# A convolution phase: one tensor's depthwise part put off through DRAM, work dealt by estimates, norms in four pieces

## The chip, the cores and the metric

The kernel runs on one core of a Trainium2 chip. The metric is device time of one execution in microseconds (us), the median of several runs; lower is better. In the profile PE is the matrix engine (PEld its weight loads), DVE the vector engine, ACT the scalar engine, POOL the GpSimd engine, and SP the engine that issues most DMAs. Each engine works through its own instructions in a fixed order, and semaphores make one wait for another.

## The reference, cut to what matters

The program is a network of three parts: a convolutional attention layer, a two-way state-space (mamba) layer and an expert layer. Only the beginning of the first part is touched. Its input is x, 64 x 64 pixels by 256 channels, normalised in groups of channels.

```python
xc = jnp.transpose(x, (0, 3, 1, 2))
qkv = jnp.concatenate([_conv(xc, W1, 0), _conv(xc, W3, 1), _conv(xc, W5, 2)], axis=1)
qkv = _conv(qkv, Wdw, 1, groups=3 * c)
q, k, v = jnp.split(qkv, 3, axis=1)
q, k, v = (heads(q), heads(k), heads(v))     # 8 heads of 32 channels
q, k = (l2n(q), l2n(k))                      # t / max(sqrt(sum(t*t)), 1e-12) over a head's channels
attn = jnp.einsum('bhnc,bhmc->bhnm', q, k) * temperature
attn = jax.nn.softmax(attn, axis=-1)
o = jnp.einsum('bhnm,bhmc->bhnc', attn, v)
...
```

So q is a 1x1, k a 3x3 and v a 5x5 convolution with 256 channels in and out; a 3x3 depthwise convolution follows each; q and k are divided, pixel by pixel, by the norm of a head's 32 channels.

## The kernel before

`conv_phase` (L174) computes q, k and v in the first 730 us and writes them to DRAM as qd, kd and vd; the attention that follows reads them from there. Channels lie on the 128 partitions, in two tiles t = 0, 1; the image is worked on in two halves of 32 rows.

The 3x3 and 5x5 convolutions are done in a Winograd manner along a row: `weights` (L285) transforms the raw weights on DVE and stores them to DRAM (uk, uv) by POOL's queue; `inputs` (L325) transforms the normalised image xpad on DVE into nine places v; PE multiplies the transformed pieces (`feed`, L421: 6 products of 6 matmuls 128x512 for a unit of k, 8 products of 10 for a unit of v; q has 4 products of 2, straight from xpad); `transform_out` (L473) reads the products on DVE and writes pad, the convolution's output with a border. Each DVE operation of these goes through the helpers at L272 and L275, each matmul product through L452 (q L444).

A unit is one tensor, half and tile. The order is four units of k, (half 0, tile 0), (0, 1), (1, 0), (1, 1), and then q and v in turn, four of each. Below, "k0" to "k3" are the four units of k, and "v0" to "v3" the stages of one v unit with the q unit before it. The loop over units (L694 to L730) does a unit in groups of two products. At each group it reads two products, calls `tick`, does a share of the previous unit's depthwise taps, and some "fills": steps of weight and input transforms that later units need, a fixed number by tensor (`share`, L722).

`depthwise` (L507) makes the nine taps of a unit: the first on ACT (L524), eight on DVE (L528), in two pieces of 12 rows of 64 pixels (128x768) or 20 rows (128x1280) each. It reads pad and writes an accumulator acc, of which there are three. For v the result is transposed in 128x128 blocks on PE (`turn`, L581) and stored. For q and k the 512-pixel chunks go into a list, from which the norms are made three chunks at a time: `norm_sums` squares on ACT and sums each head's 32 channels with one matmul per chunk into 32 partitions of a shared bank; one tick later `norm_inverse` takes the maximum with 1e-24 (L558, DVE), the root (L559, ACT) and the reciprocal (L560, DVE) of the 96x512 tile, and one matmul per chunk spreads the result back over the 128 channels, with the temperature for q (`pick_q`); another tick later `norm_apply` (L568) multiplies, stores, and begins the next three chunks. `later` (L594) and `tick` (L597) hold this lag.

The orders on the engines are the order in which this code issues the instructions (`manual_schedule`). `feed` keeps up to three products issued ahead of the one that is read, in four PSUM banks (a_pcv), and loads the transformed weights u by SP's queue three ahead (L430). `load_raw` (L279) brings raw weights in by POOL's queue into one buffer ("wr"). A pool of six buffers (a_t) holds small temporaries: wx and wo of the weights, c (ACT's copy of a product), sq, qo and vs.

## Time and profile before

| | us |
|---|---|
| median of three runs | 4381.84 |
| the three runs | 4381.84, 4389.78, 4381.30 |
| the profiled execution | 4368.56 |
| its span on the core | 4366.8 |
| convolution phase (first attention matmul at) | 730.2 |
| attention, to about | 2018 |
| mamba, to about | 4060 |

The profiled execution is 13.3 us below the median, and 1.8 us of it lie outside the span. Mean granted clock of PE over the span is 0.904 of full speed. In the tables of instruction groups a row gives line, engine, operation, output and inputs, shapes and count, then the busy time and the mean duration of one in ns, then the idle time of the engine just before them with what ended it. In the tables of time windows a row gives for each engine its busy microseconds and, in brackets, how many instructions. In a timeline a row gives the start, the duration of a run of like instructions, and in square brackets how long the engine had been idle before and what released it.

### The profile page before, as it was taken

To read this page: it belongs to the slowest core of one execution; us is meant where nothing else is said; L and a number is where in the kernel's file an instruction comes from. 1 tells how busy PE (TensorE), PEld (TensorE's weight loads), DVE (VectorE), ACT (ScalarE), POOL (GpSimd) and SP (SyncE) were. 2 spreads that over 40 slices of the span, in tenths; PEclk is the share of its full clock that TensorE was granted. 3 is DMA by queue.
4 is the path that set the end of the run, shared out by engine and by line. 5 is a ranking of instruction groups with operands and counts; after the bars stand their busy time and mean duration, and the time that the engine had idled before them with its cause. 6 is when DMAs were issued, how large, how long until landed. Compare 5 with 4: busy or idle time off the path is not lost. (4 is left out here: it accounts for less than half of the span.)

```text
span 4366.8 us, 43278 instructions
## 1 busy us (share of the span) xinstructions
PE 3693.8 (85%) x15072; PEld 1180.6 (27%) x15072; DVE 3600.9 (82%) x2976; ACT 2685.7 (62%) x4175; POOL 1563.3 (36%) x1051
## 2 busy tenths in 40 slices
PE   4659895999999999997878788888788788876698
PEld 2224341222222222222222222222222222221243
DVE  6887876888879879778899999999999999999311
ACT  1012223888788888776677777777777777774122
POOL 2210000000000000002677677776767777776000
PEclk9879996999999999998888989989888898977799
DMA  4322223000000000003332334443323334332121
GB/s 148 125 77 93 75 79 129 4 30 11 25 23 18 16 23 18 11 23 118 104 108 98 103 124 119 123 119 107 127 82 124 124 114 118 120 109 84 63 63 37
DMA packets 150243, 351.18 MB, mean 80 GB/s; under 512 B 35461, under 2 KB 44421, under 8 KB 149502
## 3 DMA queue, kind: packets, MB, share of 16 engines
q1 hardware_dynamic: 139214, 313.17, 23.1%
q0 software_dynamic: 10800, 35.14, 2.3%
q8 instruction: 120, 1.97, 0.2%
q14 instruction: 109, 0.89, 0.1%
HBM read 268.69 MB, written 79.56 MB: 80 GB/s over the span
## 5 line engine op out<-in xcount | busy, mean ns | idle before, releaser
L1669 POOL TENSOR_TENSOR dbx<-dtxr,b 128x1024 f32<-128x1024 f32 x512 | 1205.8, 2360 | 467.7 <-DVE da L1677 320.7
L1677 DVE TENSOR_TENSOR_SCAN da<-da,state,dbx 128x1024 f32<-128x1024 f32 x512 | 1203.2, 2350 | 62.0 <-ACT state L1700 33.6
L960 ACT ACTIVATE e<-sc 128x1024 f32<-128x1024 f32 x1024 | 992.8, 1023 | 204.7 <-PE sc L953 161.2
L881 DVE TENSOR_TENSOR s<-s,e 128x1024 f32<-128x1024 f32 x768 | 880.6, 1216 | 44.7 <-ACT e L960 44.2
L1659 ACT ACTIVATE da<-dtr,aneg 128x512 f32<-128x512 f32 x1024 | 708.3, 692 | 36.0 <-DMA dtr<-dtd 3.8
L953 PE MATMUL sc<-q,kS 32*128 32x512 f32 x4096 | 653.6, 644 | 20.4 <-DMA kS<-kd 11.4
L1682 DVE TENSOR_TENSOR h<-da,c 128x1024 f32<-128x1024 f32 x512 | 627.2, 1225 | 37.7
L888 PE MATMUL av<-e,vT 128*32 128x512 f32 x4096 | 549.8, 608 | 3.7 <-ACT o L894 3.7
L1709 PE MATMUL y<-h,sel 128*32 128x512 f32 x2048 | 442.0, 675 | 130.9 <-DVE h L1682 130.7
L132 POOL TENSOR_TENSOR ln_few<-ln_few,minus_half 128x4 f32<-128x4 f32 x29 | 29.4, 1015 | 1417.8 <-DMA ln_few<-ln_row 1417.8
L452 PE MATMUL cv<-v,u 128*128 128x512 f32 x928 | 422.2, 615 | 64.4 <-DVE pad L272 27.4
L953 PEld LDWEIGHTS sc<-q,kS 32*128 32x128 f32 x4096 | 211.3, 183 | 466.9 <-issue 244.4
L1250 PE MATMUL mm<-u,win 128*128 128x512 f32 x496 | 267.2, 688 | 72.0 <-DMA u<-ud 52.4
L1700 ACT COPY state<-da 128x2 f32<-128x2 f32 x511 | 80.5, 158 | 362.5 <-DVE h L1682 360.0
L452 PEld LDWEIGHTS cv<-v,u 128*128 128x128 f32 x928 | 182.1, 198 | 302.9 <-issue 230.9
L528 DVE SCALAR_TENSOR_TENSOR acc<-pad,wdw_s,acc 128x768 f32<-128x768 f32 (+1 forms) x192 | 244.5, 1279 | 19.4 <-ACT acc L524 13.3
L1294 PE MATMUL mm<-xp,taps 128*128 128x512 f32 x480 | 221.3, 609 | 6.0 <-DVE m L1441 5.1
L881 DVE TENSOR_TENSOR s<-e 128x1024 f32<-128x1024 f32 x128 | 150.8, 1219 | 71.6 <-ACT e L960 71.4
L888 PEld LDWEIGHTS av<-e,vT 128*32 128x32 f32 x4096 | 81.3, 108 | 396.6 <-issue 379.0
L1709 PEld LDWEIGHTS y<-h,sel 128*32 128x32 f32 x2048 | 60.4, 114 | 468.5 <-DVE h L1682 292.8
L1250 PEld LDWEIGHTS mm<-u,win 128*128 128x128 f32 x496 | 104.2, 221 | 244.8 <-issue 127.0
L504 ACT COPY pad<-pad 128x480 f32<-128x480 f32 x12 | 7.1, 594 | 214.2 <-DVE pad L272 214.1
(338 smaller groups left out, 3747.3 us busy)
## 6 DMA issues: line engine op xcount, KB each, us to landing
dtr<-dtd SPq DMA_DIRECT2D x128, 512.0 KB
dtxr<-dtd SPq DMA_DIRECT2D x128, 512.0 KB
b<-bcd SPq DMA_DIRECT2D x64, 256.0 KB
c<-bcd SPq DMA_DIRECT2D x64, 256.0 KB
dtd<-dt SPq DMA_DIRECT2D x64, 256.0 KB
dtd<-few SPq DMA_DIRECT2D x64, 256.0 KB
u<-uv SPq DMA_DIRECT2D x24, 640.0 KB
u<-ud SPq DMA_DIRECT2D x16, 512.0 KB
```

What stands on the lines that cost most here:

```text
L452: nc.tensor.matmul(rows4(ps), u[:, dy, P * ci : P * ci + P], v[:, dy : dy + HR, ci, :], start=dy + ci == 0, stop=dy == k - 1 and ci == CT - 1,
L528: nc.vector.scalar_tensor_tensor(o, src, w_ap, o, ALU.mult, ALU.add)
L881: nc.vector.tensor_tensor(z, x, y, ALU.add)
L888: nc.tensor.matmul(g.av[32 * h : 32 * h + 32, :], vT[:, kb, P * t + 32 * h : P * t + 32 * h + 32], es[h // 2][:, h % 2, :], start=kb == 0, ...
L953: nc.tensor.matmul(ps[h // 2][:, h % 2, :], kS[r, t, P * kb : P * kb + P], q_t[r, t, :], start=True, stop=True,)
L960: nc.scalar.activation(e, ps[i], AF.Exp)
L1250: nc.tensor.matmul(ps, win[d][:, t, P * e : P * e + P], u[:, t, ::-1] if d else u[:, t, :], start=t == 0, stop=t == CT - 1,)
L1659: nc.scalar.activation(da[:, v, :], dts[i, e, j][0][:, v, :], AF.Exp, scale=aneg[i % 2][:, a : a + 1])
L1669: nc.gpsimd.tensor_tensor(u, dts[i, e, j][1], bcs[i, k][0][:, None, :].to_broadcast([P, 2, N]), ALU.mult)
L1677: nc.vector.tensor_tensor_scan(da, da, u, state[i % 2][:, 4 * e + j, k : k + 1], ALU.mult, ALU.add)
L1682: nc.vector.tensor_tensor(h, da, bcs[i, k][1][:, None, :].to_broadcast([P, 2, N]), ALU.mult)
L1709: nc.tensor.matmul(ys[i, e][32 * j : 32 * j + 32, :], cx.sel, hs[n + j // 2][:, j % 2, :], start=False, stop=k == SQ - 1,)
```

## The change

All of it lies in `conv_phase`, which gets a scratch tensor in DRAM, kc, of two tiles of 64 rows.

- k's depthwise part is put off. A unit of k ends with its output in pad, without border work; ACT's queue stores pad to kc. A new generator `depthwise_k(t)` later fetches blocks of 16 rows and their two neighbours back by SP's queue into kr (two buffers, shared with the raw weights), and makes the nine taps in pieces of 128x1024. It starts only when the weights of v's second tile are ready.
- Raw weights are loaded by SP's queue into the same two buffers, one piece ahead, instead of by POOL's into one.
- Work is dealt by estimated times: T adds up an estimate of the time that DVE and PE have been given, from sizes (`spent`) and a cost per product (COST); `ahead` issues fills, and then put-off taps, until DVE's estimate has come up to that of the next product. It takes the place of `share`.
- `tick` is called at each product read, at each fourth put-off tap, and while a new accumulator waits for an old one's chunks to be normed (`new_acc`), and no longer once a group.
- The norms are four steps instead of three, each a tick after the other. The sums of a chunk are four matmuls of 128 pixels each with the squares as stationary operand, so they lie with pixels on partitions, 128x4 each; maximum, root and reciprocal work on 128x48; ACT copies the result out to 128x512 (rx); four matmuls against the identity bring it back for each chunk. The temperature is applied in `norm_apply`. The setup of `pick` and `pick_q` goes.
- The pool a_t has five buffers instead of six; sq and rx have a pool of three of their own.

The diff, cut to its core:

```diff
...
-        tp = ctx.enter_context(tc.tile_pool(name="a_t", bufs=6))
+        tp = ctx.enter_context(tc.tile_pool(name="a_t", bufs=5))
         accp = ctx.enter_context(tc.tile_pool(name="a_acc", bufs=3))
+        kp = ctx.enter_context(tc.tile_pool(name="a_kp", bufs=2))
+        sp = ctx.enter_context(tc.tile_pool(name="a_sq", bufs=3))
         pcv = ctx.enter_context(tc.tile_pool(name="a_pcv", bufs=4, space=PSUM))
         pms = ctx.enter_context(tc.tile_pool(name="a_pms", bufs=1, space=PSUM))
...
+        nc.vector.tensor_reduce(heads, cx.ident.rearrange("p (a b) -> p a b", b=32), AX.X, ALU.add)
...
+        T = {"PE": 0.0, "DVE": 0.0}
...
+        def spent(out):
+            n = 1
+            for m in out.shape[1:]:
+                n *= m
+            T["DVE"] += 0.146 + 0.00105 * n
...
-        def load_raw(kind, co, dy, pool=rp, tag="wr"):
+        def load_raw(kind, co, dy, pool=kp, tag="kr"):
             n = KS[kind]
             r = pool.tile([P, 5, C], FP, name="wr", tag=tag)
-            nc.gpsimd.dma_start(out=r[:, 0:n, :], in_=RAW[kind][co, :, :, dy, :].rearrange("x p c -> p x c"))
+            nc.sync.dma_start(out=r[:, 0:n, :], in_=RAW[kind][co, :, :, dy, :].rearrange("x p c -> p x c"))
             return r
...
             def stand(i, s):
                 V[kind, half, i] = place[s].rearrange("p (r t j) -> p r t j", t=CT, j=TX)
                 where[kind, half, i] = s
+                since[kind, half, i] = T["DVE"]
...
                             )
+                done[n] = T["PE"] = max(T["PE"], since.get((kind, half, i), 0.0), done.get(("free", n - 4), 0.0)) + COST[kind]
                 at["job"] += 1
...
         def product():
...
                 feed()
             n = at["used"]
             at["used"] += 1
+            T["DVE"] = done["free", n] = max(T["DVE"], done[n])
+            tick()
             (kind, half, t), i = jobs[n]
...
+        accs, put_off = [], []
+        def step_put_off():
+            while put_off and ("v", 1) in ready:
+                r = next(put_off[0], None)
+                if r is not None:
+                    return r
+                put_off.pop(0)
+            return False
+        def acc_free():
+            return len(accs) < 3 or not accs[-3]["left"]
+        def new_acc(left):
+            while not acc_free():
+                if not step_put_off():
+                    tick()
+            accs.append({"left": left})
+            return accp.tile([P, (H - LAG) * W], FP, name="acc", tag="acc"), accs[-1]
         def depthwise(kind, half, t, pad):
             row0, n = (LAG, H - LAG) if half else (0, LAG)
             ch = {"q": 0, "k": CT, "v": 2 * CT}[kind] + t
-            dst = accp.tile([P, (H - LAG) * W], FP, name="acc", tag="acc")
+            dst, log = new_acc(1 if kind == "v" else n // ROWS)
...
                     o, src, w_ap = piece(b, tap)
+                    spent(o)
                     nc.vector.scalar_tensor_tensor(o, src, w_ap, o, ALU.mult, ALU.add)
                     yield
                 if kind == "v":
                     turn(dst, t, row0 * W // P, n * W // P // 2 * b, n * W // P // 2)
             if kind != "v":
                 c0 = row0 // ROWS
...
+                log["left"] = 0
+        def depthwise_k(t):
+            KB = 16
+            def fetch(b):
+                x = kp.tile([P, KB + 2, 6, TX], FP, name="kr", tag="kr")
+                lo, hi = max(KB * b - 1, 0), min(KB * b + KB + 1, H)
+                at0 = lo - (KB * b - 1)
+                if at0:
+                    nc.gpsimd.memset(x[:, 0], 0.0)
+                if hi - lo + at0 < KB + 2:
+                    nc.gpsimd.memset(x[:, KB + 1], 0.0)
+                nc.sync.dma_start(out=x[:, at0 : at0 + hi - lo], in_=kc[t][:, lo:hi])
+                return x
+            x, dst, log = fetch(0), None, None
+            yield True
+            for b in range(H // KB):
+                if b % 2 == 0:
+                    while not acc_free():
+                        yield False
+                    dst, log = new_acc(2 * KB // ROWS)
+                y = fetch(b + 1) if b + 1 < H // KB else None
+                o = dst[:, KB * W * (b % 2) : KB * W * (b % 2 + 1)]
+                for tap in range(9):
+                    dy, dx = divmod(tap, 3)
+                    src = x[:, dy : dy + KB, dx : dx + 4, :].rearrange("p h s j -> p h (s j)")
+                    w_ap = wdw[:, 9 * (CT + t) + tap : 9 * (CT + t) + tap + 1]
+                    o3 = o.rearrange("p (h w) -> p h w", w=W)
+                    if tap == 0:
+                        nc.scalar.activation(o3, src, AF.Copy, scale=w_ap)
+                    else:
+                        spent(o)
+                        nc.vector.scalar_tensor_tensor(o3, src, w_ap, o3, ALU.mult, ALU.add)
+                        if tap % 4 == 0:
+                            tick()
+                        yield True
+                x = y
+                for j in range(KB // ROWS):
+                    rows_left.append((o[:, N * j : N * j + N], "k", t, KB // ROWS * b + j, log))
                 if not busy:
                     norm_sums()
...
             busy[:] = chunks
             if not chunks:
                 return
+            sqs = []
+            for a, *_ in chunks:
+                sqs.append(sp.tile([P, N], FP, name="sq", tag="sq"))
+                nc.scalar.activation(sqs[-1], a, AF.Square)
+            later(lambda: norm_add(chunks, sqs))
+        def norm_add(chunks, sqs):
             ps = pms.tile([P, N], FP, name="ps", tag="ps0")
-            for j, (a, _, _, _) in enumerate(chunks):
-                sq = tp.tile([P, N], FP, name="sq", tag="t")
-                nc.scalar.activation(sq, a, AF.Square)
-                nc.tensor.matmul(ps[32 * j : 32 * j + 32, :], heads, sq, start=True, stop=True)
+            for j, sq in enumerate(sqs):
+                for i in range(N // P):
+                    nc.tensor.matmul(
+                        ps[:, 16 * j + 4 * i : 16 * j + 4 * i + 4], sq[:, P * i : P * i + P], heads,
+                        start=True, stop=True,
+                    )
+            T["PE"] += 1.0 * len(chunks)
             later(lambda: norm_inverse(chunks, ps))
         def norm_inverse(chunks, ps):
-            n = 32 * len(chunks)
-            rn = rp.tile([P, N], FP, name="rn", tag="rn")
-            nc.vector.tensor_scalar(rn[0:n, :], ps[0:n, :], 1e-24, None, ALU.max)
-            nc.scalar.activation(rn[0:n, :], rn[0:n, :], AF.Sqrt)
-            nc.vector.reciprocal(rn[0:n, :], rn[0:n, :])
+            n = 16 * len(chunks)
+            rn = rp.tile([P, 48], FP, name="rn", tag="rn")
+            nc.vector.tensor_scalar(rn[:, 0:n], ps[:, 0:n], 1e-24, None, ALU.max)
+            nc.scalar.activation(rn[:, 0:n], rn[:, 0:n], AF.Sqrt)
+            nc.vector.reciprocal(rn[:, 0:n], rn[:, 0:n])
+            xs = []
+            for j in range(len(chunks)):
+                xs.append(sp.tile([P, 16, 32], FP, name="rx", tag="sq"))
+                nc.scalar.copy(xs[-1], rn[:, 16 * j : 16 * j + 16, None].to_broadcast([P, 16, 32]))
+            later(lambda: norm_back(chunks, xs))
+        def norm_back(chunks, xs):
             back = []
-            for j, (_, kind, t, _) in enumerate(chunks):
+            T["PE"] += 1.6 * len(chunks)
+            for j, x in enumerate(xs):
+                x = x.rearrange("p (i h) c -> p i (h c)", h=4)
                 back.append(pms.tile([P, N], FP, name="ps", tag=f"ps{j}"))
-                r = slice(32 * j, 32 * j + 32)
-                nc.tensor.matmul(back[j], (pick_q[t] if kind == "q" else pick)[r, :], rn[r, :], start=True, stop=True)
+                for i in range(N // P):
+                    nc.tensor.matmul(back[j][:, P * i : P * i + P], x[:, i, :], cx.ident, start=True, stop=True)
             later(lambda: norm_apply(chunks, back))
         def norm_apply(chunks, back):
-            for (a, kind, t, c), ps in zip(chunks, back):
-                plus(a, a, ps, ALU.mult)
+            for (a, kind, t, c, log), ps in zip(chunks, back):
+                log["left"] -= 1
                 if kind == "q":
+                    nc.vector.scalar_tensor_tensor(a, ps, temp[:, t : t + 1], a, ALU.mult, ALU.mult)
                     s = tp.tile([P, N], FP, name="qo", tag="t")
                     nc.scalar.copy(
                         s.rearrange("p (h j r) -> p h r j", j=TX, r=4), a.rearrange("p (h r j) -> p h r j", r=4, j=TX)
                     )
                     a = s
+                else:
+                    plus(a, a, ps, ALU.mult)
                 nc.gpsimd.dma_start(out=(qd if kind == "q" else kd)[t][:, N * c : N * c + N], in_=a)
             norm_sums()
...
-            def all_weights(pieces):
+            def all_weights():
+                pieces = [("k", 1, dy) for dy in range(3)] + [("v", t, dy) for t in range(CT) for dy in range(5)]
                 r = load_raw(*pieces[0])
                 for n, p in enumerate(pieces):
-                    yield from (True for _ in weights(*p, r))
-                    if n + 1 < len(pieces):
-                        r = load_raw(*pieces[n + 1])
+                    r, r_next = (load_raw(*pieces[n + 1]) if n + 1 < len(pieces) else None), r
+                    yield from (True for _ in weights(*p, r_next))
                     if p[2] == KS[p[0]] - 1:
                         ready.add(p[0:2])
+            every = all_weights()
+            def until(*key):
+                while key not in ready and step(every):
+                    yield True
             fills = [
-                first, all_weights([("k", 1, dy) for dy in range(3)]), inputs("k", 1),
-                all_weights([("v", 0, dy) for dy in range(5)]), inputs("v", 0),
-                all_weights([("v", 1, dy) for dy in range(5)]), inputs("v", 1),
+                first, until("k", 1), inputs("k", 1), until("v", 0), inputs("v", 0), until("v", 1), inputs("v", 1),
             ]
...
+            def ahead(lag):
+                while True:
+                    n = min(at["used"] + 1, len(jobs) - 1)
+                    end = done.get(n, T["PE"])
+                    if T["DVE"] + lag >= end or not (step_fill() or step_put_off()):
+                        return
+                    feed()
             before = None
...
+                if kind == "k":
+                    pass
+                elif half:
...
                     step(main)
                     feed()
-                    tick()
                     for _ in range(-(-18 // groups)):
                         step(before)
-                    for _ in range(share[kind]):
-                        step_fill()
+                    ahead(0.5)
                     feed()
                 drain(main)
                 drain(before)
+                before = None
+                if kind == "k":
+                    nc.scalar.dma_start(out=kc[t][:, HR * half : HR * half + HR], in_=pad[:, 1 : HR + 1])
+                    if half:
+                        put_off.append(depthwise_k(t))
+                    continue
                 if not half:
                     nc.scalar.copy(edge, pad[:, LAG : LAG + 9])
                 before = depthwise(kind, half, t, pad)
+            while put_off:
+                step(before)
+                if not step_put_off():
+                    tick()
             drain(before)
             while events:
                 tick()
...
```

## The prediction

> **What bounds the kernel now.** I read the forty slices first, then the convolution phase in stretches cut at the last product read of each unit, then its groups by shape, then single stretches of the timeline; the chain that ended last covers only the closing microseconds and says nothing. All work after the phase is the same in both kernels, instruction for instruction on every engine, so only the first 730 us count.
>
> ```profile
> PE   4659895999999999997878788888788788876698
> DVE  6887876888879879778899999999999999999311
> ```
> A slice is 109 us. In the first three PE is about half idle, in the next three nearly full; in the seventh, the phase's tail, it drops again.
>
> Busy time by stage (columns: us; PE; weight loads; DVE; ACT; POOL; PE clock; DMA share; GB/s). Rows 1 to 4 are k's units, 5 to 8 a v unit each with the q units dealt between, 9 the tail:
> ```profile
> 36.00:89.50 53.50, 35.39 (x72) 15.11 (x72) 26.66 (x41) 1.17 (x2) 8.06 (x15) 0.88 0.26 82
> 89.50:145.50 56.00, 43.96 (x97) 19.45 (x98) 49.50 (x81) 4.83 (x7) 12.53 (x23) 0.90 0.48 155
> 145.50:217.40 71.90, 41.13 (x85) 16.46 (x84) 57.44 (x99) 7.72 (x12) 17.27 (x31) 0.76 0.38 121
> 217.40:298.90 81.50, 34.54 (x69) 13.22 (x69) 66.15 (x89) 7.76 (x11) 15.02 (x28) 0.67 0.29 94
> 298.90:384.80 85.90, 82.77 (x195) 33.99 (x195) 74.73 (x68) 17.00 (x27) 3.74 (x9) 0.95 0.22 75
> 384.80:494.60 109.80, 90.52 (x224) 37.64 (x223) 88.62 (x80) 19.53 (x30) 5.61 (x11) 0.93 0.23 76
> 494.60:578.60 84.00, 82.18 (x203) 34.42 (x202) 61.65 (x66) 23.14 (x35) 5.99 (x13) 0.97 0.25 83
> 578.60:664.90 86.30, 81.82 (x207) 35.81 (x205) 64.36 (x55) 20.63 (x30) 5.07 (x10) 0.98 0.20 70
> 664.90:730.20 65.30, 15.37 (x43) 5.44 (x43) 40.57 (x45) 15.29 (x22) 5.97 (x11) 0.54 0.24 84
> ```
> The reader should see two regimes: k stages (263 us, PE busy 155) wait for DVE and weights; v stages (366 us, PE busy 337) are bound by PE. DVE work taken out of k stages buys time; put into v stages it is free only up to some 20 us each, the idle of DVE there.
>
> DVE prices:
> ```profile
> L528 DVE SCALAR_TENSOR_TENSOR acc<-pad,wdw_s,acc 128x1280 f32<-128x1280 f32 x96 | 147.9, 1546 | 9.0 <-ACT acc L524 5.5 <-DVE acc L528 0.5
> L528 DVE SCALAR_TENSOR_TENSOR acc<-pad,wdw_s,acc 128x768 f32<-128x768 f32 x96 | 96.7, 1012 | 10.4 <-ACT acc L524 7.8
> L560 DVE RECIPROCAL rn<-rn 96x512 f32<-96x512 f32 x9 | 30.1, 3349 | 13.2 <-ACT rn L559 13.2
> ```
> A tap is 1.55 or 1.01 us, so 1.28 for the new 128x1024; a reciprocal 3.35, twelve in all.
>
> PE in a v stage, and DVE at the start of one:
> ```profile
> 394.67 25.91 PE L452 MATMUL cv<-v,u 128*128 128x512 f32 x60
> 420.51 1.06 PE L551 MATMUL ps<-sq,heads 128*32 128x512 f32 x6
> 421.50 0.66 PE L587 MATMUL tr<-ident,acc 128*128 128x128 f32 x4
> ```
> ```profile
> 584.13 0.69 DVE L558 TENSOR_SCALAR rn<-ps 96x512 f32<-96x512 f32 x1 [4.59 <-PE ps L551]
> 588.24 3.35 DVE L560 RECIPROCAL rn<-rn 96x512 f32<-96x512 f32 x1 [3.42 <-ACT rn L559]
> 591.51 9.39 DVE L528 SCALAR_TENSOR_TENSOR acc<-pad,wdw_s,acc 128x1280 f32<-128x1280 f32 x6
> ```
> A matmul of four-byte numbers is two records: 60 are three v products, 8.6 us each (k 5.1, q 1.7). Three chunks' sums are one packed group, 1.06 us; a 128x128 record costs 0.11. One norm chain stands before v3's own taps, which start 13 us after the stage does (591.5 against 578.6).
>
> **The change part by part**, walked along the instruction orders of both builds (these are fixed per engine).
>
> *k's taps put off.* 64 taps of 1.28 us = 82 leave stages k1 to v0 and return between v1 and v3: same elements, no DVE time saved. DVE by stage, from these rows, after (before): k0 22 (29), k1 30 (50), k2 29 (60), k3 30 (68), v0 69 (76), v1 91 (91), v2 104 (63), v3 86 (65), tail 33 (42). k1's first product waits for its weights, computed after k0: about 99.5 us. Eighteen products at 5.14 give 192; DVE by its sums 188 plus two waits of 6 for raw weights. I take 201.5 as the end of k3: 97 early. The stores are four issues of some 0.4 us on ACT (the size of SP's issues), which is 8 us busy in such a stage; they follow ACT's own copies into pad, so ACT waits for nothing new. The eight fetches of 0.85 MB start after v1's weights, long after the stores. On SP the third stands before v1's last two u loads and waits for the first block's taps, which DVE does before v1's first read: no price.
>
> *Raw weights by SP, one piece ahead.* Ten issues of 0.9 us leave POOL, which is never bound here. On SP they stand between u loads, and a load that waits for its buffer holds the u loads behind it. Bounds: nothing, if DVE frees buffers in time (gaining the row "wr" of waits, 34 us), or two stages held 19 us each: k3 then ends about 240. I take 12 us, two waits at the measured size:
> ```profile
> DVE wx L275 <- DMA wr<-in_w: 34.2, 8, 6.1
> ```
> (A row of the waits: 34.2 us in all, 8 times, 6.1 the longest.)
>
> *Norms in four pieces.* Each chunk becomes 4 sums and 4 backs of 128 columns or fewer, 16 records. By 0.107 (row below) to 0.11 that is 1.76 us against 0.7 packed; 27 chunks before v3 ends make +28 on PE. DVE loses 12 reciprocals of 3.35, some 37 us; ACT gains 27 copies of 0.55 (0.55 the 512-column copy; 1.1, the permuting copy, is the upper end), in an engine 17 to 23 busy in 84. The upper price of small matmuls is the cold one:
> ```profile
> 4053.97 1.95 PE L158 MATMUL tl<-mean_mat,hn 128*128 128x1 f32 x16 [2.40 <-ACT hn L153]
> 4090.18 3.57 PE L158 MATMUL tl<-mean_mat,u 128*128 128x1 f32 x16 [2.46 <-ACT u L153]
> ```
> 0.21 a record, 3.4 us a chunk.
>
> The Trainium skill, "TensorE: Matmul & The Clock Gate", section "Back-to-back issue gap", gives 81 ns as sustained spacing at 128 columns. By it, as an estimate, a chunk would be 1.3 us and the PE sum some 12 us less; the row shows 0.11, so the sum does not use it.
>
> *Chains at the start of v2 and v3.* This decides. New ticks stand in every product read, and a new accumulator is asked for only when an old one's chunks are all normed: the order puts whole chains ahead of the stage's own sixteen taps. From v1's last product read (zero): last tap 1.5; three squares to 3.5; sums to 6; back matmuls stand behind the last q product and v2's first, to 16.5; backs and three applies to 21; then sums of the next pair stand behind v2's second and third product, to 36.3; two chains of two (sums 1.8, inverse 1.0, copies 1.1, backs 1.8, applies 1.2, hand-offs 0.7) of 7.6 each: 51.5. Before it was 14 (508.85 against 494.6). Then 16 taps of 1.01 end at 67.7, and transposes follow. PE has no product to work on from 36 to 67, as all four product banks are full. After that DVE has 104 - 24 = 80 of work and some 10 of stalls: v2 lasts 158 (before 84). v3 alike: one pair behind v3's first product, three chunks behind its second and third: 43 (13), 16 taps of 1.55 to 68, then 54 of DVE and 20 of stalls: 142 (86).
>
> *Work dealt by estimates, five temporaries for six, setup cut by 2.4 us of DVE.* The first only shifts fills (in the orders already); the second can hold an ACT copy by at most a store's landing, 2.6 us in the DMA rows; the third is the 2 us by which k0 ends earlier.
>
> *Sum.* k3 201.5; v0 +75.4 (PE) = 277; v1 +111, as before (DVE 91, PE 88, each waiting for the other) = 388; v2 546; v3 688; tail 51.5, before 55, as the last two chains lose 6.4 of reciprocals and gain copies and matmuls: 739.5. Before, the tail ends and attention follows:
> ```profile
> 718.82 1.29 DVE L275 TENSOR_TENSOR acc<-acc,ps 128x512 f32<-128x512 f32 x2 [2.22 <-PE ps L565]
> 730.18 2.09 PE L953 MATMUL sc<-q,kS 32*128 32x512 f32 x8 [11.36 <-DMA kS<-kd]
> ```
> Ten us for the last store and kS: 749.6, that is +20. Small matmuls in the starts and the tail (17 chunks; all cold, +28) I price a fifth cold: +6. In all +26 on the profiled execution's 4368.6, which lies 13 under the median: 4395 there, 4408 on the median's scale. So DVE gives back in two starts (37 + 30) and two DVE-bound remainders what the k stages gain.
>
> **Rivals.**
> *Faster: no stalls outside the two starts.* Place: v1 and what follows each start. v1 would take its 91, v2 67.7 + 80, v3 68 + 54: 20 + 10 + 20 less, 4358. For it: dealing waits until PE is expected to be ahead, and 51 us of DVE work are gone. Against: in v1 before, neither engine is over 83% busy. It decides once stalls fall by over 35 of the 50. Were the starts' chains hidden as well, stages would be 75, 91, 104, 91 by the larger engine, about 4277; I hold that excluded by the orders, as a square can only follow its last tap.
>
> *The put-off does not shorten the k stages:* raw weights on SP hold the u loads, k3 ends near 240: 38 more, 4446. For it: DMA share is already 0.48 in k1; against: landing is 4.9 us.
>
> *Colder PE.* All 17 chunks cold are +22 beyond the +6; three restarts after idling cost 1.85 each (one group of 48 records took 22.45 in k0, where 0.43 a record makes 20.6): 4436.
>
> *About even:* half of the 50 us of stalls gone: 4383.
>
> **How the numbers follow.** Chance of the walk (4385 to 4435) 0.60; k stages held or PE cold (4435 to 4450) 0.14; even 0.09; faster 0.17. A measurement tells 0.2%, 8.8 us. Slower: 0.57 of the first and the second whole, 0.71; same 0.12; faster 0.17. The range runs from half of the faster rival's gain beyond its 4358, 4345, to the held k stages, 4446.
>
> **What would show it.** Right: k3's last read near 200 us; no reciprocal above 0.5; DVE idle some 40 us at the start of v2 and 30 of v3, ending on PE's ps; first attention matmul near 755. Wrong: if k3 ends at 240, the SP step failed; if own taps of v2 start under 30 us, the chains; if v1 takes 95, the stalls.

## The result, and the profile after

The changed kernel takes 4444.08 us (median of four runs, 4440.06 to 4446.34) against 4383.36 for the one before: 1.0135 times as long, 95% interval 1.0123 to 1.0147, so 60.7 us slower. The forecast was slower, 4408; the direction held and the range (up to 4446) just holds the time, but the rise is more than twice the 26 us forecast. The profiled execution of after took 4440.06 us, its span is 4438.2, and its first attention matmul starts at 794.1 us (before: 730.2). So 63.9 of the 71.4 us between the two profiled spans lie in the convolution phase, where all sides of the forecast had the loss; the other 7.5 lie behind it, in work that the change does not touch.

The forty slices of after, PE alone (a slice is now 111 us):

```profile
PE   3998665899999999998788888878888888876698
```
PE is at 9 in slices 2 and 3, where it was at 6 and 5 before: the k stages did get shorter. In slices 5 and 6 it is at 6, where it had been at 8 and 9. The gain is given back there.

The same by stage, cut at the last product read of each unit (columns as before: us, then busy time of PE, weight loads, DVE, ACT, POOL, then PE clock, DMA share, GB/s; rows k0 to k3, v0 to v3, tail):

```profile
36.00:88.20 52.20, 37.57 (x71) 15.48 (x69) 17.25 (x21) 1.17 (x2) 0.00 (x0) 0.84 0.12 38
88.20:142.70 54.50, 35.37 (x76) 15.55 (x77) 29.72 (x47) 2.26 (x4) 7.49 (x14) 0.78 0.46 152
142.70:185.60 42.90, 40.64 (x95) 17.83 (x94) 28.19 (x72) 2.27 (x5) 12.84 (x24) 1.00 0.71 231
185.60:215.50 29.90, 25.99 (x58) 11.14 (x57) 29.59 (x40) 2.25 (x5) 3.39 (x7) 0.95 0.61 212
215.50:296.80 81.30, 77.42 (x177) 34.13 (x176) 67.04 (x115) 9.79 (x15) 15.46 (x31) 0.96 0.49 168
296.80:411.40 114.60, 96.38 (x269) 49.13 (x268) 91.73 (x88) 23.31 (x37) 5.23 (x11) 0.87 0.24 77
411.40:579.30 167.90, 120.42 (x396) 72.22 (x395) 105.42 (x114) 39.43 (x65) 9.43 (x20) 0.77 0.21 76
579.30:733.10 153.80, 102.98 (x333) 58.18 (x331) 87.50 (x82) 30.74 (x48) 8.59 (x19) 0.79 0.14 49
733.10:794.10 61.00, 22.46 (x100) 19.73 (x101) 34.14 (x44) 17.95 (x27) 6.14 (x12) 0.56 0.26 91
```
k3 ends 83.5 us earlier than before (215.5 against 299.0). v2 is twice as long (167.9 against 84.0) and v3 nearly so (153.8 against 86.3), and in neither is an engine busy for more than 72% of it: DVE and PE take turns. Their PE clock is 0.77 and 0.79, where it was 0.97 and 0.98.

DVE at the start of v2, from the timeline of after:

```profile
429.93 2.54 DVE L646 SCALAR_TENSOR_TENSOR acc<-ps,temp,acc 128x512 f32<-128x512 f32 x3 [12.03 <-PE ps L639]
450.62 0.19 DVE L623 TENSOR_SCALAR rn<-ps 128x32 f32<-128x32 f32 x1 [18.16 <-PE ps L612]
462.07 0.19 DVE L623 TENSOR_SCALAR rn<-ps 128x32 f32<-128x32 f32 x1 [5.27 <-PE ps L612]
468.09 16.70 DVE L538 SCALAR_TENSOR_TENSOR acc<-pad,wdw_s,acc 128x768 f32<-128x768 f32 x16
```
This answers to the rows of before in which one chain stood ahead of a stage's taps. Now three stand there, waiting in turn for PE, and the stage's own taps begin 56.7 us after it (468.09 less 411.4); before it was 14.

PE there, with the second half of that start as a row of the stage table (its clock is the third number from the end):

```profile
448.68 1.84 PE L612 MATMUL ps<-heads,sq 128*128 128x4 f32 x16
458.40 3.58 PE L612 MATMUL ps<-heads,sq 128*128 128x4 f32 x16 [2.39 <-ACT sq L605]
```
```profile
450.50:468.10 17.60, 11.17 (x49) 10.46 (x48) 3.90 (x9) 7.52 (x12) 1.62 (x3) 0.53 0.17 68
```
The same sixteen small records (the sums of two chunks) take 1.84 us behind v's products and 3.58 alone, that is 0.11 and 0.22 each; the back matmuls at 452.2 and 463.7 take 3.79 and 3.78, so 0.24 each. The clock granted to PE is 1.00 in the 18 us before 450.5 and 0.53 in the 17.6 after.

SP, POOL and PE at the start of k1:

```profile
61.60 40.05 SPq L266 DMA_DIRECT2D wr<-in_w  x5
102.10 3.45 SPq L415 DMA_DIRECT2D u<-uk  x3
```
```profile
99.96 1.07 POOL L277 DMA_DIRECT2D uk<-wo  x2 [5.96 <-DVE wo L259]
```
```profile
107.33 23.05 PE L437 MATMUL cv<-v,u 128*128 128x512 f32 x46 [19.86 <-DMA u<-uk]
```
SP stands 40 us in raw loads that wait for buffers, with the loads of k1's transformed weights behind them. That looks like the cause of k1's late first product, but it is not: POOL stores the last piece of that product's weights only at 99.96, when DVE has made it, and the product starts 7.4 us after that store. In three runs below, two of them with raw loads by POOL and two with work dealt earlier, it starts 8.7 to 8.9 us after the same store.

### The profile page after: what moved, and what is told of

It is laid out like the page before. It is cut to its first block, busy times and chain, and to the rows that moved or that the text cites. A ratio compares the mean times of both kernels' runs of the same rounds, so it can differ in the third digit from the quotient of the medians.

```text
span 4438.2 us, 44134 instructions
## 1 busy us (share of the span) xinstructions
PE 3740.1 (84%) x15454; PEld 1265.0 (29%) x15454; DVE 3566.3 (80%) x2963; ACT 2697.2 (61%) x4205; POOL 1548.3 (35%) x1035
## 5 line engine op out<-in xcount | busy, mean ns | idle before, releaser
L1060 ACT ACTIVATE e<-sc 128x1024 f32<-128x1024 f32 x1024 | 992.5, 1023 | 201.5 <-PE sc L1053 157.7
L1350 PE MATMUL mm<-u,win 128*128 128x512 f32 x496 | 271.6, 698 | 75.6 <-DMA u<-ud 53.8
L1809 PEld LDWEIGHTS y<-h,sel 128*32 128x32 f32 x2048 | 59.7, 113 | 465.9 <-DVE h L1782 296.6
L1350 PEld LDWEIGHTS mm<-u,win 128*128 128x128 f32 x496 | 105.9, 225 | 250.4 <-issue 129.6
L538 DVE SCALAR_TENSOR_TENSOR acc<-pad,wdw_s,acc 128x768 f32<-128x768 f32 (+1 forms) x128 | 163.7, 1284 | 12.5 <-ACT acc L533 8.9
L1394 PEld LDWEIGHTS mm<-xp,taps 128*128 128x128 f32 x480 | 88.6, 192 | 145.1 <-issue 97.5
```

The source lines that it names most:

```text
L1060: nc.scalar.activation(e, ps[i], AF.Exp)
L1350: nc.tensor.matmul(ps, win[d][:, t, P * e : P * e + P], u[:, t, ::-1] if d else u[:, t, :], start=t == 0, stop=t == CT - 1,)
L1394: nc.tensor.matmul(ps, taps[d][:, 4 * e + k, :], xp[:, e, k : k + N], start=k == 0, stop=k == 3)
L1809: nc.tensor.matmul(ys[i, e][32 * j : 32 * j + 32, :], cx.sel, hs[n + j // 2][:, j % 2, :], start=False, stop=k == SQ - 1,)
```

## The experiments

Two theories stood at the beginning. Theory F was the forecast's: whole norm chains are forced ahead of v2's and v3's own taps. Rival N: the norms in four pieces cost the time wherever they stand. (Rival S, the raw weights on SP's queue, came with the profile after.) Reading the orders again showed why the chains are forced: the generator `depthwise_k` puts the two chunks of a finished block on the list only when it is next stepped. By then q's five chunks are on the list, the buffer wanted for v's accumulator is the one of k's block, and all seven chunks must be normed first. Below, "phase end" is the start of the first attention matmul, 794.1 in after and 730.2 in before; it leaves out what differs between runs in the rest of the program. Ratios are to the kernel before, run on the same chip.

**Early entry of finished chunks.**

```diff
@@ depthwise_k
+                        if tap == 8:
+                            for j in range(KB // ROWS):
+                                rows_left.append((o[:, N * j : N * j + N], "k", t, KB // ROWS * b + j, log))
+                            if not busy:
+                                norm_sums()
                         if tap % 4 == 0:
                             tick()
                         yield True
                 x = y
-                for j in range(KB // ROWS):
-                    rows_left.append((o[:, N * j : N * j + N], "k", t, KB // ROWS * b + j, log))
-                if not busy:
-                    norm_sums()
```


> After's kernel, but the two finished chunks of a put-off block go into the list of chunks at the block's last tap, not when the generator is next stepped. Theory F (forced chains): in after v2's own sixteen taps wait 56.8 us and v3's 46.2, because the buffer that v2's accumulator takes over still holds two chunks of k that entered the list late, behind five chunks of q, so that three chains run ahead of the taps. With the early entry one chain of three remains ahead of v2's taps: they start about 20 us after the stage instead of 56.8, v3's about 35 instead of 46; the time falls by 35 to 50, to 4394 to 4409 on the median's scale. Rival N (the norms' small matmuls and copies themselves, wherever they stand): the same records and copies run, so the time stays within 10 of 4444. Rival S (raw weights on SP's queue): within 10 of 4444 too.

Measured: 4422.29, ratio 1.0098 (1.0078 to 1.0118); phase end 774.5, that is 19.6 earlier. DVE at v2's start:

```profile
450.04 16.71 DVE L538 SCALAR_TENSOR_TENSOR acc<-pad,wdw_s,acc 128x768 f32<-128x768 f32 x16 [4.63 <-ACT acc L533]
```
One chain is left ahead of them (its three multiplications stand at 442.9), and own taps start 28.7 us after the stage (421.3) instead of 56.7. So the cause of the forced chains is shown. The time gained is about half of the 35 to 50 expected, and the put-off taps moved too: v2 became 12 shorter (155.9) with 39 of them in it instead of 32, v3 18 shorter (136.0) with 9 instead of 16, and v1 10 longer with a third chain. v3's own taps start 45.4 us after its stage, where about 35 was expected. F is right in kind and too large.

**Raw weights by POOL's queue.**

```diff
-            nc.sync.dma_start(out=r[:, 0:n, :], in_=RAW[kind][co, :, :, dy, :].rearrange("x p c -> p x c"))
+            nc.gpsimd.dma_start(out=r[:, 0:n, :], in_=RAW[kind][co, :, :, dy, :].rearrange("x p c -> p x c"))
```


> After's kernel, raw weights issued by POOL's queue, with the same two buffers and the same loading ahead. Theory F with its term for SP: in after SP stands 40 us (61.6 to 101.7) in five raw loads that wait for buffers, and k1's first product starts at 107.3; now the u loads of k1 go out as soon as the weights are stored, first product 95 to 99, and v stages as before: 8 to 14 less, 4430 to 4436. Rival S (SP's queue is the main loss, in all k stages): k3's last read moves from 215 to below 190 and the time falls by 25 or more, under 4419. It could also gain nothing, if the first product waits for the stores of its weights by POOL, now behind raw loads on that queue: 4444.

Measured: 4426.63, ratio 1.0114 (1.0096 to 1.0132); phase end 781.0, 13.1 earlier. k1's first product came no earlier (110.5), so the wait that I named is not the one that paid here: k2 and v0 became shorter (31.1 against 42.9, 76.0 against 81.3). From 140 to 216 us DVE waits 13.0 us for raw weights in after, where they stand on SP between loads of u, and 1.5 us here. SP's queue costs some 13 us, over several stages; rival S's 25 it does not.

**Norms as before** (with the setup of `pick` and six buffers in a_t again).

```diff
@@ norm_sums, norm_inverse: three steps, packed
-                    nc.tensor.matmul(
-                        ps[:, 16 * j + 4 * i : 16 * j + 4 * i + 4], sq[:, P * i : P * i + P], heads,
-                        start=True, stop=True,
-                    )
+                nc.tensor.matmul(ps[32 * j : 32 * j + 32, :], heads, sq, start=True, stop=True)
...
-                    nc.tensor.matmul(back[j][:, P * i : P * i + P], x[:, i, :], cx.ident, start=True, stop=True)
+                nc.tensor.matmul(back[j], (pick_q[t] if kind == "q" else pick)[r, :], rn[r, :], start=True, stop=True)
```


> After's kernel with the norms of before: three steps, packed sums into 32 partitions, reciprocal on 96x512, no copies by ACT. Eight put-off taps move into the tail by the estimates, 10 us of DVE. Theory F: chains still stand ahead of the starts, v2's own taps at 50 to 60, v3's at 30 to 45; the packed matmuls save PE time mostly where it is idle, reciprocals cost 3.35 each again: 4425 to 4455. Rival N (norms in four pieces are the loss): the time falls by 40 or more, to 4404 or less.

Measured: 4439.95, ratio 1.0148 (1.0121 to 1.0174); phase end 791.3. v2 is 26 shorter (141.8) and v3 20 (134.2), but the tail is 45 longer (105.9, with 69 us of DVE in it instead of 34), as the order, with fewer ticks, leaves sixteen put-off taps and further chains to it (eight taps were expected). Inconclusive on the price of the pieces, since the order changed with them; as a whole the norms of before are no better here.

**k not put off.**

```diff
-                if kind == "k":
-                    nc.scalar.dma_start(out=kc[t][:, HR * half : HR * half + HR], in_=pad[:, 1 : HR + 1])
-                    if half:
-                        put_off.append(depthwise_k(t))
-                    continue
                 if not half:
                     nc.scalar.copy(edge, pad[:, LAG : LAG + 9])
                 before = depthwise(kind, half, t, pad)
```


> After's kernel without the put-off: k's depthwise part is made from pad in the next stage, as before, nothing goes through kc; everything else (dealing by estimates, raw weights by SP, norms in four pieces, ticks) as in after. Theory F: the 82 us of taps return to the k stages, k3's last read near 290 to 300; no chunk enters late, so v2's and v3's own taps start 15 to 25 after their stages, which last about 90 each: 4375 to 4400. Rival (the put-off gains what it should, and the rest of the change loses): the time rises by 40 or more, to 4484 or more.

Measured: 4499.7, ratio 1.0275 (1.0252 to 1.0298); phase end 851.3, 57 later than after. My forecast for it missed, for a reason that its waits in v0 (235.7 to 445.3) show:

```profile
PE cv L437 <- DVE v L259: 51.4, 1, 51.4
```
With k's own taps on DVE, its estimate runs ahead, and fewer fills are dealt in the k stages: from k1 to k3 DVE makes 52 operations on weights and 12 on inputs, in after 97 and 27. PE then waits for v's inputs, and v0 takes 209.6. So with work dealt in this way the put-off gains. What it would gain against k's taps in place and fills dealt in time, no run here shows.

**Dealing more.** One number; the lines in `product` only let it go on where weights become ready in the last step of the fills, and stand in the kernel without the put-off and in all with more dealing:

```diff
-                assert step_fill()
+                more = step_fill()
                 feed()
+                assert more or at["used"] in ms
...
-                    ahead(0.5)
+                    ahead(-10)
```


> After's kernel, with one number changed: DVE may be dealt work until its estimate is 10 us past the next product's end, instead of 0.5 us short of it. By the order 45 of the 64 put-off taps then stand in v0 and 19 in v1, none in v2 and v3 (after: 3, 13, 32, 16). Theory O (order): the time is lost because put-off taps with their chains stand in v2 and v3, where DVE and PE then take turns; now v2 lasts 95 to 110 (after 168), v3 90 to 105 (154), v0 grows by some 45 us of taps and chains to 110 to 140 (81): 4444 falls by 50 to 90, to 4354 to 4394. Rival N (the norms in four pieces cost the time wherever they stand): 4444 falls by 20 at most, v2 and v3 stay above 120 each.

Measured: 4417.17, ratio 1.0081 (1.0055 to 1.0107); phase end 771.7, 22.5 earlier. v2 and v3 fall to 97.3 and 101.5, as expected, but the taps cost nearly the same again where they now stand:

```profile
207.50:351.10 143.60, 102.08 (x319) 56.01 (x318) 102.23 (x114) 25.90 (x42) 8.44 (x20) 0.82 0.31 109
351.10:512.20 161.10, 109.87 (x353) 61.48 (x353) 107.42 (x107) 30.45 (x51) 8.19 (x17) 0.81 0.17 60
```
v0 and v1 (these two rows) have DVE and PE each busy 102 to 110 us of 144 and 161. A stage with put-off taps and their chains takes far longer than its busier engine needs, whichever stage it is (18 us of v0 turn out below to be a queue's). Theory O's gain of 50 to 90 is not there. k1's first product starts at 82.6 instead of 107.3, with the raw loads still on SP: DVE makes its weights earlier.

**Four edits together, norms of before** (dealing, early entry, raw weights by POOL, norms of before).

```diff
...
-                    ahead(0.5)
+                    ahead(-10)
...
+                        if tap == 8:
...
-            nc.sync.dma_start(out=r[:, 0:n, :], in_=RAW[kind][co, :, :, dy, :].rearrange("x p c -> p x c"))
+            nc.gpsimd.dma_start(out=r[:, 0:n, :], in_=RAW[kind][co, :, :, dy, :].rearrange("x p c -> p x c"))
...
...
+                nc.tensor.matmul(ps[32 * j : 32 * j + 32, :], heads, sq, start=True, stop=True)
```


> After's kernel with four edits together: dealt 10 us past, early entry of finished chunks, raw weights by POOL's queue, norms of before. Theory O: k's put-off is a gain once nothing of it stands in v2's and v3's starts: k3's last read near 200 (DVE fills earlier, no SP hold), v0 105 to 125, v1 105 to 120, v2 95 to 110, v3 86 to 90, tail 55, first attention matmul 660 to 710 against before's 730: 4310 to 4365, faster than before. Rival P (the put-off can't pay, as its taps and loads only move): first attention matmul at 725 or later, 4375 or more.

Measured: 4403.21, ratio 1.0060 (1.0037 to 1.0084); phase end 760.8. A miss: v0 146.8, v1 131.6, v2 126.7. By its numbers this is rival P; two of the runs with the fetches by ACT's queue below end the phase before 725 with k put off, so P does not hold in general.

**The same with norms in four pieces.**

```diff
-                nc.tensor.matmul(ps[32 * j : 32 * j + 32, :], heads, sq, start=True, stop=True)
+                    nc.tensor.matmul(
+                        ps[:, 16 * j + 4 * i : 16 * j + 4 * i + 4], sq[:, P * i : P * i + P], heads,
+                        start=True, stop=True,
+                    )
```


> As the run with all four edits, but with after's norms in four pieces. The difference of the two is the norms' own price where no put-off taps stand beside them in v2 and v3. Theory O with its PE sum: 27 chunks at 1.06 us more on PE, part of it in stages that PE bounds, against 12 reciprocals less on DVE in a DVE-bound v0: 5 to 30 slower than with the norms of before. Rival N: 40 or more slower. Against the run with only the dealing changed it tells what SP's queue and the late entry still cost: 10 to 25 faster than that.

Measured: 4391.43, ratio 1.0030 (1.0014 to 1.0046); phase end 742.0. With four pieces it is 19 faster at the phase end than with the norms of before, where both theories had it slower; fourteen taps that the order leaves in v2 there, and none here, are the visible difference (v2 95.6 against 126.7). The three small edits are worth 52 us together. Its v0 still lasts 139.2, and in it:

```profile
234.32 10.53 DVE L584 SCALAR_TENSOR_TENSOR acc<-kr,wdw_s,acc 128x1024 f32<-128x1024 f32 x8 [24.93 <-ACT acc L581]
```
```profile
209.79 17.49 SPq L415 DMA_DIRECT2D u<-uv  x3
227.38 17.86 SPq L563 DMA_DIRECT2D kr<-kc  x3
```
DVE waits 24.9 us for a first tap of ACT, which waits for a fetch of kc that stands on SP behind loads of u. This is again one queue for loads of two kinds.

**Dealing still more** (as the four edits with the norms of before).

```diff
-                    ahead(-10)
+                    ahead(-20)
```


> As the run with all four edits, but dealt 20 us past instead of 10: by the order 17 put-off taps stand in k3, 47 in v0, none later; the fills stand in k0 and k1. Theory O: DVE then bounds the k stages, PE idles there and runs colder, and v0 holds less: within 20 either way of the run with 10, 4300 to 4380. If the time rises by 30 or more, the k stages do not have the DVE time that I take them to have.

Measured: 4431.34, ratio 1.0120 (1.0081 to 1.0159); phase end 789.3, 28.5 later than with 10. k3 ends at 258.3 (195.8 with 10): k3 then holds 17 put-off taps and two chains and lasts 78.0, with DVE busy for 53.8 of it and PE for 44.6. PE waits 18.9 us in it for squares, and ACT in turn 24.4 for the taps that it squares. So the time goes to taps and chains in one stage again; DVE is idle for 24 us of it.

**Small matmuls doubled.** In after's kernel, the disputed cost twice:

```diff
+                    for _ in range(2):
                         nc.tensor.matmul(
                             ps[:, 16 * j + 4 * i : 16 * j + 4 * i + 4], sq[:, P * i : P * i + P], heads,
...
+                    for _ in range(2):
                         nc.tensor.matmul(back[j][:, P * i : P * i + P], x[:, i, :], cx.ident, start=True, stop=True)
```


> After's kernel with each small matmul of the norms (sums and backs) issued twice, the output unchanged. In after's timeline these matmuls take 41 us of sums and 48 us of backs, 90 us for 32 chunks, 2.8 a chunk. The second copy costs between 56 us (0.11 a record) and 90 us of PE. The rise tells what part of that stands on the path: theory F with the cold price (chains in the starts and the tail are exposed, 17 chunks) 35 to 65 us, 4479 to 4509; if they are hidden beside DVE's work, under 15; if all of it is on the path, 75 or more.

Measured: 4501.8, ratio 1.0280 (1.0250 to 1.0310); phase end 853.8, 59.7 later. By stage against after: v1 10.8, v2 27.3, v3 12.7, tail and start of attention 10.5 longer. The originals take, in after:

```profile
L639 PE MATMUL ps<-ident,rx 128*128 128x128 f32 x256 | 48.4, 370 | 41.7 <-ACT rx L629 41.7
L612 PE MATMUL ps<-heads,sq 128*128 128x4 f32 x256 | 41.2, 294 | 13.9 <-ACT sq L605 13.9
```
89.6 us for 32 chunks, 2.8 a chunk, against 18.9 + 10.8 + 8.7 = 38.4 for the packed ones of before by the same view. With the second copy the two rows are 78.5 and 88.8 us, so 77.7 more, and the end moves by 59.7: three quarters of what was added is on the path. That the first copy weighs as much is inferred. What N says of their size is right; that they were the whole loss is not, as the last run below keeps them and beats both kernels.

**Fetches by ACT's queue** (on the run with three edits and norms in four pieces).

```diff
-                nc.sync.dma_start(out=x[:, at0 : at0 + hi - lo], in_=kc[t][:, lo:hi])
+                nc.scalar.dma_start(out=x[:, at0 : at0 + hi - lo], in_=kc[t][:, lo:hi])
```


> As the run with dealing, early entry and raw weights by POOL (norms in four pieces), with the eight fetches of kc issued by ACT's queue instead of SP's. In that run DVE stood 24.9 us in v0 for a first tap on ACT that waited for a fetch, which stood on SP behind u loads that waited for their buffers. Theory Q (that stall is the queue): it goes, v0 139 falls to 110 to 120, the time from 4391 to 4365 to 4378, about before's or faster. Rival (DVE and PE take turns anyway, the stall only moves): 4385 to 4395, v0 stays above 130.

Measured: 4368.94, ratio 0.9983 (0.9971 to 0.9994): slightly faster than before. Phase end 721.0, 21.1 earlier than with the fetches on SP; v0 is 121.4 (139.2). Theory Q holds: the 24.9 us wait is 2.4 now, and it did not move elsewhere (no later stage is more than 0.2 longer). The first tap's row, and what DVE waits for in its v stages then:

```profile
210.76 10.53 DVE L584 SCALAR_TENSOR_TENSOR acc<-kr,wdw_s,acc 128x1024 f32<-128x1024 f32 x8 [2.43 <-ACT acc L581]
```
```profile
DVE acc L648 <- PE ps L641: 47.3, 4, 17.1
```
Four chains, three of them at a stage's start, wait 47 us for back matmuls that stand on PE behind whole products of v.

**Fetches by ACT's queue, norms of before, dealt 14 past.**

```diff
-                    ahead(-10)
+                    ahead(-14)
...
-                nc.sync.dma_start(out=x[:, at0 : at0 + hi - lo], in_=kc[t][:, lo:hi])
+                nc.scalar.dma_start(out=x[:, at0 : at0 + hi - lo], in_=kc[t][:, lo:hi])
```


> All four edits with the norms of before, dealt 14 us past, and the fetches by ACT's queue. By the order 10 put-off taps in k3, 47 in v0, 7 in v1, none later. Theory O: v0 125 to 135, v1 105 to 112 (before 110), v2 and v3 84 to 90 each, tail 55: first attention matmul 680 to 715 against 730: 4330 to 4367, faster than before. Rival T (turns: each chain in a stage with put-off taps costs both engines, so 64 taps and eleven chains in one stage take 150 or more): 4380 or more.

Measured: 4404.28, ratio 1.0053 (1.0030 to 1.0076); phase end 758.5. v1 to v3 go back to 112.8, 101.1 and 94.9, but v0 takes 165.0 with 47 taps and six chains in it, and DVE is busy for 122.8 of that, PE for 109.4: rival T. Chains and taps crowded into one stage cost both engines.

**Backs issued with the inverse, for q's chains** (on the run with the fetches by ACT and norms in four pieces).

```diff
-            later(lambda: norm_back(chunks, xs))
+            if chunks[0][1] == "q":
+                norm_back(chunks, xs)
+            else:
+                later(lambda: norm_back(chunks, xs))
```


> As the run with the fetches by ACT's queue and norms in four pieces, but a chain that begins with q's chunks issues its back matmuls with its inverse, not a tick later. By PE's order they then stand behind one v product in v1 instead of two, and behind none in v2 and v3 instead of one or two. In that run DVE waits 47 us in four places for these backs and PE 50 us for the taps behind them. Theory F (a chain ahead of a stage's own taps costs by the products that stand between its pieces): own taps of v2 25 us after the stage falls to 14 to 17, v3's likewise, v1's 33 to 24 to 28; the time from 4369 to 4340 to 4355. Rival (PE then stands idle for ACT's copies as long as DVE did before): within 8 of 4369.

Measured: 4359.06, ratio 0.9951 (0.9934 to 0.9968); phase end 711.3, 9.7 earlier than without and 18.9 earlier than in before. PE at v2's start (460.9):

```profile
463.28 5.12 PE L614 MATMUL ps<-heads,sq 128*128 128x4 f32 x24
468.26 3.76 PE L429 MATMUL cv<-xpad,wq 128*128 128x512 f32 x4
471.81 2.91 PE L644 MATMUL ps<-ident,rx 128*128 128x128 f32 x24
```
Only a q product is left between sums and backs; own taps start 19.7 us after the stage (480.6) instead of 24.8, and in v3 18.5 instead of 24.9; 14 to 17 was expected. v2 lasts 95.8 with and without the edit all the same, and most of the gain stands in v3 (93.5 against 100.8). The time came 4 us short of the gain expected, but this version beats both kernels: 23 us faster than before, 0.5%, and some 80 faster than after (phase end 82.8 earlier).

## Why the prediction was right or wrong

The direction, the place and the kinds of wait were right. What failed is the sum: nearly every term in it is too small, and 60.7 us were lost where it had 26. The walk put the first attention matmul at 749.6 and 6 us of cold matmuls on top; it came at 794.1.

- *k stages.* Right that they shorten, and by k's taps; but k3 ended at 215.5 for 201.5, the largest miss of the sum. k1's first product came at 107.3 for 99.5. It did wait for its weights, as the text has it, but among them DVE stood 5.8 us for a raw weight, a wait that the text put into DVE's sum for the k stages and not here. The u loads' wait behind raw loads on SP, which the text names too, has no part in it: dealing alone brought this product to 82.6 with the raw loads on SP, and raw loads by POOL alone left it at 110.5. Eighteen products then took 100.2 us for 92.5, at a clock of 0.78 in k1, and 95.1 with the raw loads on POOL.
- *v0 and v1.* 81.3 for 75.4 and 114.6 for 111. v0 takes 76.0 with the raw loads on POOL, so its miss is SP's queue, which the text priced in the k stages alone; v1's stays open.
- *Start of v2 and v3.* Right in place and cause: own taps 56.7 us after the stage for 51.5, and 46.1 for 43. What is missing is the cold price: the last pair's sums and backs took 3.58 and 3.78, where the walk had 1.8 each.
- *Rest of v2 and v3.* 94.5 and 82.5 us after the end of the taps, for 90 and 74. I had added stalls of 10 and 20 to DVE's work by feeling. DVE and PE take turns where put-off taps and chains stand together; the run that moved the taps to v0 and v1 shows it there too, so it is not a property of these two stages.
- *The cold price.* The text held 17 chunks in the starts and the tail at 1.76 us and "a fifth cold", 36 us in all, 6 of them for the cold. The sums and backs of these chunks take 47.4 us in after (18.6 in v2's start, 12.0 in v3's, 16.9 in the tail), 2.8 a chunk: 17.5 for the cold where the sum had 6. The share was a guess, and the bound of +28 for all of them stood in the text, under "colder PE" at 4436; the truth lies midway between the two.
- *Tail.* 56.9 for 51.5, given back by 6 us in the start of attention, as 4.1 us instead of 10 passed from the last norm to the first matmul.

The rival with no stalls (4358) failed on its own condition: stalls did not fall, they grew. The rival of 4446 has nearly the measured time by luck, as its way there did not happen: k3 ended at 215.5, not at 240. The sum of the terms missed is 14 + 5.9 + 3.6 + 9.9 + 11.8 + 5.4 - 6.1 = 44.5 us, which is the walk's whole distance from the trace; the 9.9 and 11.8 are v2 and v3, their starts and rests together.

Three readings in the text are slightly off and move no term: the row at 4053.97 gives 0.112 us a record, not 0.107; ACT's copy of 512 columns takes 0.58 us in before, not 0.55 (the new one 0.61); and the sums of DVE by stage lie 0.5 to 2.6 us above the busy columns of before's table.

The Trainium skill's sustained spacing at 128 columns ("TensorE: Matmul & The Clock Gate", section "Back-to-back issue gap", 81 ns) does not describe these pieces: they took 0.11 us a record behind products and 0.22 to 0.24 alone, so the sum had to go the other way from the warm row.

What made the change slow is shown by taking it out piece by piece: late entry of chunks 20 us alone, raw loads on SP 13, dealing too late 23, the three together 52, fetches behind u loads a further 21, and q's backs behind products 10. Without these, k put off through DRAM with norms in four pieces is 23 us faster than before. What the norms in four pieces cost by themselves is not isolated, as each run with the norms of before also moves put-off taps. Why DVE and PE overlap so poorly in a stage with put-off taps (v1 still lasts 146.0 with 108.5 of DVE and 110.2 of PE in the best version) stays open.

## What to carry to other kernels

Taking work off the engine that bounds one stage pays only if the stage that gets it has that time left and no chain between engines comes with it: here 84 us were gained in four stages and 147 lost in the next four and the tail. Every hand-over between two in-order engines here waited for whatever was issued between its pieces, so a dependent piece issued one step later can cost the products in between; in v2 of the last run it cost nothing, in v3 7 us. Before DMAs of two kinds share a queue, ask which of them waits for a buffer, because the others wait with it: 24.9 us here. But a queue that stands still need not be what holds the work up; look when the data behind it was ready.

## What the runs showed of the hardware that was not expected

Small matmuls between idle stretches are dear: sixteen records took 1.84 us behind products, with a granted clock of 1.00, and 3.6 to 3.8 us alone, with 0.53, so such a chain pays twice for them. Standing behind a product is not enough: in the last run 24 sums took 5.12 us (0.21 each) behind a q product that itself came after 11.1 us of idling. By stage, the granted clock is 1.00 in k2, where PE is 95% busy, and 0.56 in the tail, where it is 37% busy.
